# Sign convolutions by halves of images, weight sums one block later, and another order in attention

## The chip, the cores and the metric

One core of one Trainium2 chip runs the whole program. The metric is the device time of a run in microseconds (us), lower is better. TensorE (PE in the profile) multiplies matrices, with its weight loads on a row of their own (PEld). VectorE (DVE), ScalarE (ACT) and GpSimd (POOL) work element by element. SyncE (SP) issues most transfers.

## The reference, cut to what matters

Four layers run one after the other on 16 images of 256 channels and 28 x 28 points, all in float32.

```python
# layer 0: convolution of signs with signs of weights, scaled, normalised, plus the input
out = _binary_activation(x)                              # forward value: sign(x)
scaling = jnp.mean(jnp.abs(weights), axis=(1, 2, 3))
bw = jnp.sign(weights)                                   # forward value
y = _sat_conv2d(out, bw, padding=1, stride=1) * scaling.reshape(1, -1, 1, 1)
# mean and variance over batch and points, then yn * gamma + beta + x

# layer 1: residual block: 3x3 convolution of signs with real weights, 1x1 convolution, two gates

# layer 2: batchnorm, sign, binconv, prelu, batchnorm, sign, binconv, prelu, batchnorm
sf = jnp.mean(jnp.abs(w), axis=(1, 2, 3), keepdims=True) # in each binconv
bw = sf * jnp.sign(w)

# layer 3: self-attention over the 784 points, then
out = jnp.einsum('cr,brn->bcn', Wp, out)
return out.reshape(B, C, H, W) + x
```

Three sign convolutions (one in layer 0, two in layer 2) need signs of 256 x 256 x 9 weights and the mean of their absolute values. The signs go into the convolution; the means are wanted only at the normalisation after it.

## The kernel before: the parts the change touches

The program runs in five stages: sign convolution 1 (layer 0), the residual stage (layer 1), sign convolutions 2 and 3 (layer 2), attention.

A sign convolution works on blocks of 16 rows. The images lie below each other in a ring of three, each followed by one row of zeros that is the lower border of one and the upper border of the next. So 16 images are 16 x 29 = 464 rows, or 29 blocks of 16 x 28 = 448 columns, and a block may begin in one image and end in the next. A block has 23 matmuls: 15 with packed weights (both halves of the output channels in one number), 6 plain ones for the last chunk of weights, and 2 that unpack.

```python
BR = 16
BN = BR * S                      # S = 28
NBLK = B * (S + 1) // BR         # 29
...
for j in range(NBLK + 1):
    if j == 0:
        sign_image(0)
    if j < NBLK:
        packed(j)                # 15 matmuls; then ScalarE and VectorE round the sum
    if j > 0:
        plain(j - 1)             # 6 matmuls, then 2 that unpack
        post(j - 1, pss[j - 1], parts(j - 1))
    ...                          # signs of the next images, as soon as the ring has room
    if j >= 2 and steps:
        steps.pop(0)()
```

`post` takes the block's statistics, in as many pieces (`parts`) as it touches images: VectorE's `bn_stats`, ScalarE's conversion, per piece. `steps` holds work on weights, one step a block. In sign convolution 1 these are seven steps that prepare the weights of the residual stage and six sums of its own weights. In sign convolution 2 they are one sum of its own and the signs and sums of the six weight chunks of sign convolution 3. (Its other sums are taken in the residual stage, where GpSimd does the adding up.) A sum is:

```python
V.tensor_reduce(ab, st.rearrange("p t o -> p o t"), AX.X, ALU.add, apply_absolute_value=True)
part = acc.tile([P, 2], F32, tag="sm", name="sumabs")
for mo in range(2):                               # sums over the partitions, on TensorE
    T.matmul(part[:, mo:mo + 1], lhsT=ab[:, mo * P:(mo + 1) * P], rhs=ones, start=True, stop=True)
V.scalar_tensor_tensor(total, part, 1.0 / K9, total, ALU.mult, ALU.add)
```

The orders on TensorE, ScalarE and VectorE are those of the program (a manual schedule). In attention, image b begins with `project(b - 2, 0)`, `scores(b, 1)`, `scores(b, 2)`; each `scores` is two matmuls and an exponential on ScalarE, with two PSUM buffers in turn. (The timelines count four instructions, x4, for the two matmuls of a sum, of a `scores` or of a `project`.) `take_values(b)`, a ScalarE copy, ends the image.

## Time and profile before

The stages are cut where the first matmul of the next stage starts in TensorE's timeline; "attention" is counted from its first scores (its first projections, from 970.68 us on, are in the row above) to the end.

| | us |
|---|---|
| run, median (1281.66 to 1283.36) | 1282.2 |
| sign convolution 1 | 200.1 |
| residual stage | 401.8 |
| sign convolution 2 | 212.9 |
| sign convolution 3 | 163.4 |
| attention | 302.2 |

Sign convolutions 2 and 3 have the same matmuls, and one takes 49.5 us longer. That is the first thing a table by stage shows.

### The profile page before, as it was taken

How to read it: one execution, taken by the hardware profiler on the slowest of the kernel's cores; microseconds unless marked ns; L12 is line 12 of the kernel's file. 1: busy time of each engine (PE TensorE's matmuls, PEld its weight loads, DVE VectorE, ACT ScalarE, POOL GpSimd, SP SyncE). 2: the span in 40 equal slices, each digit the busy share in tenths (PEclk: the TensorE clock that was granted, in tenths of full speed). 3: DMA queues.
4: the chain of work that ended last, by engine and by line, in shares of the span. 5: the costliest groups of instructions: out<-in, count | busy, mean ns of one | idle time of the engine just before them, and what ended most of it. 6: DMA issues, size and time to landing. Idle time of an engine off the chain costs nothing.

```text
span 1280.3 us, 15397 instructions
## 1 busy us (share of the span) xinstructions
PE 1158.5 (90%) x5808; PEld 931.2 (73%) x5812; DVE 818.1 (64%) x1539; ACT 711.3 (56%) x1067; POOL 137.4 (11%) x137
## 2 busy tenths in 40 slices
PE   6967999999999999985665999999999999999996
PEld 5856888999989999973554888688885545555452
DVE  2833348899999999964334566566666456555655
ACT  4632544676666765655323454455547766776653
POOL 1000000010000000000000000000001432433232
PEclk9978999999999999997877999999999999999998
DMA  7531422133222221103701000000001354445511
GB/s 285 177 136 38 151 91 78 61 113 101 67 110 76 84 103 54 48 29 154 284 25 52 25 1 1 1 1 1 1 1 63 89 151 139 126 114 151 151 77 78
DMA packets 25968, 111.61 MB, mean 87 GB/s; under 512 B 3552, under 2 KB 6304, under 8 KB 25888
## 3 DMA queue, kind: packets, MB, share of 16 engines
q1 hardware_dynamic: 20432, 80.85, 18.2%
q0 software_dynamic: 5456, 29.71, 7.9%
q8 instruction: 48, 0.79, 0.3%
q14 instruction: 32, 0.26, 0.1%
HBM read 65.59 MB, written 44.96 MB: 86 GB/s over the span
## 4 chain that ended last, share of the span: by engine, by line
PE 61%; DVE 13%; ACT 8%; issue 2%; POOL 1%; DMA 0%; ACTq 0%; DVEq 0%; POOLq 0%
PE cv L243 21%; PE cv L567 14%; PE av L992 6%; PE sc L971 6%; PE mi L956 3%; PE sm L1032 3%; PE mi L1042 2%; PE cv L262 2%; DVE p L811 1%; DVE x L696 1%; ACT y L642 1%; DVE x L651 1%; DVE l_parts L698 1%; ACT rn L527 1%; DVE xs L559 1%
## 5 line engine op out<-in xcount | busy, mean ns | idle before, releaser
L243 PE MATMUL cv<-ring,wpk 128*128 128x448 f32 x1305 | 324.7, 405 | 18.7 <-DVE unpack L394 8.8
L567 PE MATMUL cv<-vs,w 128*128 128x392 f32 x1536 | 303.2, 356 | 9.1 <-DVE y L600 7.2
L243 PEld LDWEIGHTS cv<-ring,wpk 128*128 128x128 f32 x1305 | 268.8, 208 | 57.1 <-issue 11.6
L567 PEld LDWEIGHTS cv<-vs,w 128*128 128x128 f32 x1536 | 287.9, 191 | 13.2 <-DVE y L600 10.0
L254 ACT ACTIVATE t<-cv,rounding 128x448 f32<-128x448 f32 x87 | 54.9, 631 | 167.1 <-PE cv L243 167.1
L811 DVE SCALAR_TENSOR_TENSOR p<-r,r,cv 128x448 f32<-128x448 f32 (+15 forms) x172 | 87.1, 506 | 80.2 <-ACT r L806 80.2
L243 PE MATMUL cv<-ring,wpl 128*128 128x448 f32 x522 | 126.6, 379 | 0.0
L255 DVE TENSOR_SCALAR up<-t 128x448 fp32r<-128x448 f32 x87 | 34.0, 391 | 144.5 <-ACT t L254 144.4
L975 ACT ACTIVATE es<-sc 112x784 f32<-112x784 f32 x112 | 87.3, 822 | 61.4 <-PE sc L971 61.3
L243 PEld LDWEIGHTS cv<-ring,wpl 128*128 128x128 f32 x522 | 99.4, 190 | 13.5
L971 PE MATMUL sc<-q,k 64*112 64x392 f32 x448 | 90.6, 518 | 6.2 <-ACT es L975 4.4
L806 ACT ACTIVATE r<-cv 128x896 f32<-128x896 f32 (+1 forms) x60 | 53.4, 893 | 57.7 <-PE cv L262 55.5
L992 PE MATMUL av<-es,va 112*64 112x392 f32 x448 | 80.8, 500 | 0.0
L963 DVE COPY k<-mi 64x784 f32<-64x784 f32 x16 | 15.6, 976 | 93.3 <-ACT q L962 93.3
L971 PEld LDWEIGHTS sc<-q,k 64*112 64x112 f32 x448 | 36.3, 174 | 47.9 <-ACT es L975 16.6
L110 DVE TENSOR_TENSOR vs<-pad 128x840 fp32r<-128x840 bf16 (+1 forms) x68 | 64.1, 975 | 0.6 <-ACT pad L538 0.5
L992 PEld LDWEIGHTS av<-es,va 112*64 112x64 f32 x448 | 29.4, 136 | 47.6 <-issue 44.8
L473 ACT CAST n<-cv 128x896 int16<-128x896 f32 (+15 forms) x43 | 27.7, 645 | 60.7 <-DVE l_parts L472 57.8
L211 PE MATMUL sumabs<-ones,ab 128*128 128x1 f32 x52 | 10.9, 313 | 55.7 <-DVE ab L208 55.7
L985 POOL TENSOR_TENSOR sum<-sum,es 112x784 f32<-112x784 f32 x32 | 60.4, 1887 | 2.5
L664 PE MATMUL cv<-z,fw 128*128 128x392 f32 x256 | 52.4, 355 | 5.1 <-ACT z L655 5.0
L681 ACT ACTIVATE u<-cv,c_bn,s_bn 128x784 f32<-128x784 f32 x31 | 31.1, 1004 | 46.3 <-PE cv L664 46.3
(229 smaller groups left out, 1702.8 us busy)
## 6 DMA issues: line engine op xcount, KB each, us to landing
xs<-in_x_dram SPq DMA_DIRECT2D x32, 784.0 KB, 4.4
x2d<-x POOLq DMA_DIRECT2D x16, 784.0 KB, 3.6
xd<-p SPq DMA_DIRECT2D x16, 784.0 KB, 3.3
out_dram<-p SPq DMA_DIRECT2D x15, 784.0 KB, 5.2
p<-x2d SPq DMA_DIRECT2D x13, 784.0 KB, 15.9
p<-x2d POOLq DMA_DIRECT2D x13, 784.0 KB, 9.0
n0d<-n POOLq DMA_DIRECT2D x16, 392.0 KB, 2.6
n<-n0d SPq DMA_DIRECT2D x16, 392.0 KB, 3.2
```

What stands on the lines that cost most here:

```text
L110: V.tensor_tensor(o, a, b, op)
L243: T.matmul(pss[j][:, mo, :BN].rearrange("p (a b) -> p a b", b=S), lhsT=lhsT, rhs=ring[:, k, r:r + BR, c:c + S], start=start, stop=stop, sk ...
L254: A.activation(r, pss[j][:, 0, :BN], AF.Identity, bias=rounding, scale=1.0 / PACK)
L567: T.matmul(ps.rearrange("p (a b) -> p a b", b=S), lhsT=w[:, k, c, u, mo * P:(mo + 1) * P], rhs=vs[:, b % 2, u, k, :, c:c + S], start=(n == 0),
L664: T.matmul(ps[:, h, :HN], lhsT=w[:, k, mo * P:(mo + 1) * P], rhs=z2[b][:, k, h * HN:(h + 1) * HN], start=(n == 0), stop=(n == 3),)
L806: A.activation(r[:, mo], ps[:, mo, :BN], AF.Relu, scale=-1.0)
L811: V.scalar_tensor_tensor(p, r[:, mo, p0:p0 + n], beta[:, mo:mo + 1], ps[:, mo, p0:p0 + n], ALU.mult, ALU.add)
L956: T.matmul(ps[:, h, :HN], lhsT=wqk[:, k, :], rhs=x[b][:, k, h * HN:(h + 1) * HN], start=(k == 0), stop=(k == 1),)
L971: T.matmul(ps[:MC, h, :HN], lhsT=k_[rows, c * MC:(c + 1) * MC], rhs=qs[b][rows], start=True, stop=True)
L975: A.activation(e, ps[:MC, :, :HN], AF.Exp, scale=0.125)
L985: (V if late else nc.gpsimd).tensor_tensor(sums[b, late], sums[b, late], e, ALU.add)
L992: T.matmul(ps[64 * h:64 * h + 64, :HN], lhsT=w, rhs=e[:, h, :], start=start, stop=stop)
```

## The change

It has three parts. Blocks become halves of images: two buffers with a padded image each take the place of the ring, and 32 blocks of 392 columns that of 29 of 448. Sums of weights come in two steps: VectorE's part in one block, TensorE's part (and the total) one block later. In attention, scores 1 goes ahead of the projection, and the `take_values` of the image before moves behind its exponential.

```diff
-    def ring_tile(pool, tag):
-        t = pool.tile([P, 2, RROWS + BR + 2, S + 2], FR, tag=tag, name="ring")
+    def float_pads(pool, tag):
+        t = pool.tile([P, 2, 2, S + 2, S + 2], FR, tag=tag, name="fpads")
 ...
                 V.tensor_reduce(ab, st.rearrange("p t o -> p o t"), AX.X, ALU.add, apply_absolute_value=True)
+            return lambda: total_up(k, g, ab)
+
+        def total_up(k, g, ab):
             part = acc.tile([P, 2], F32, tag="sm", name="sumabs")
 ...
-            for j in range(NBLK + 1):
+            for j in range(2 * B + 1):
                 if j == 0:
                     sign_image(0)
-                if j < NBLK:
+                if j < 2 * B:
                     packed(j)
                 if j > 0:
                     plain(j - 1)
-                    post(j - 1, pss[j - 1], parts(j - 1))
+                    post(j - 1, pss[j - 1])
+                if j == 0:
+                    sign_image(1)
+                elif j % 2 == 0 and j // 2 + 1 < B:
+                    sign_image(j // 2 + 1)
 ...
-                if j >= 2 and steps:
-                    steps.pop(0)()
+                if late:
+                    late()
+                late = steps.pop(0)() if j >= 2 and steps else None
 ...                                    (the same two lines in the residual stage; then post of layer 0)
-                for at, b, r0, r1, p0 in parts:
-                    n = (r1 - r0) * S
 ...
-                    for mo in range(2):
-                        V.bn_stats(mom.part(at, mo), ps[:, mo, p0:p0 + n])
-                    A.copy(ns[b][:, :, r0 * S:r1 * S], ps[:, :, p0:p0 + n])
 ...
+                for mo in range(2):
+                    V.bn_stats(mom.part(j, mo), ps[:, mo, :HN])
+                A.copy(ns[b][:, :, h * HN:(h + 1) * HN], ps[:, :, :HN])
 ...                                    (attention)
+            scores(b, 1)
+            if b > 0:
+                take_values(b - 1)
             if b > 1:
                 project(b - 2, 0)
-            scores(b, 1)
             sum_up(b, 1)
             scores(b, 2)
 ...
-                take_values(b)
                 if b > 0:
                     normalize(b - 1)
```

More of the change, by code (lines that the diff above doesn't have):

```diff
@@ L46 @@
 EPS = 1e-5
-BR = 16
-BN = BR * S
-NBLK = B * (S + 1) // BR
-RING = 3
-RROWS = RING * (S + 1)
 PACK = 4095.0
@@ L91, in conv_seq_kernel @@
     nc.gpsimd.memset(ones, 1.0)
-    def ring_tile(pool, tag):
-        t = pool.tile([P, 2, RROWS + BR + 2, S + 2], FR, tag=tag, name="ring")
-        nc.gpsimd.memset(t[:, :, 0::S + 1, :].bitcast(F32), 0.0)
-        for c in (0, S + 1):
-            nc.gpsimd.memset(t[:, :, :, c:c + 1].bitcast(F32), 0.0)
+    def float_pads(pool, tag):
+        t = pool.tile([P, 2, 2, S + 2, S + 2], FR, tag=tag, name="fpads")
+        for i in (0, S + 1):
+            nc.gpsimd.memset(t[:, :, :, i:i + 1, :].bitcast(F32), 0.0)
+            nc.gpsimd.memset(t[:, :, :, :, i:i + 1].bitcast(F32), 0.0)
         return t
@@ L221, in run @@
             f()
-            s()
+            return s()
         return [lambda f=f, s=s: run(f, s) for f, s in zip(first, second)]
@@ L230, in split2, with sign_layer @@
         tt(dsts[1], st, dsts[0].bitcast(F32), ALU.subtract)
-    def sign_layer(ring, w, temp, sign, post, steps, moments):
-        pss = [None] * NBLK
-        bs = [None] * NBLK
+    def sign_layer(pads, w, temp, sign, post, steps, moments):
+        pss = [None] * 2 * B
+        bs = [None] * 2 * B
         def product(j, mo, lhsT, n, t, start, stop, again=False):
@@ L241, in product @@
             r, c = divmod(3 * g + t, 3)
-            r += BR * j % RROWS
+            r += HR * (j % 2)
             T.matmul(
-                pss[j][:, mo, :BN].rearrange("p (a b) -> p a b", b=S), lhsT=lhsT,
-                rhs=ring[:, k, r:r + BR, c:c + S], start=start, stop=stop, skip_group_check=again,
+                pss[j][:, mo, :HN].rearrange("p (a b) -> p a b", b=S), lhsT=lhsT,
+                rhs=pads[:, j // 2 % 2, k, r:r + HR, c:c + S], start=start, stop=stop, skip_group_check=again,
             )
@@ L253, in packed @@
             r, bs[j] = temp("t1"), temp("up", FR)
-            A.activation(r, pss[j][:, 0, :BN], AF.Identity, bias=rounding, scale=1.0 / PACK)
+            A.activation(r, pss[j][:, 0, :HN], AF.Identity, bias=rounding, scale=1.0 / PACK)
             V.tensor_scalar(bs[j], r, -ROUND, None, ALU.add)
@@ L262, in plain @@
                 T.matmul(
-                    pss[j][:, mo, :BN], lhsT=unpack[mo], rhs=bs[j], start=False, stop=True, skip_group_check=(mo == 0)
+                    pss[j][:, mo, :HN], lhsT=unpack[mo], rhs=bs[j], start=False, stop=True, skip_group_check=(mo == 0)
                 )
-        count = 0
-        def parts(j):
-            nonlocal count
-            at, out = BR * j, []
-            while at < BR * (j + 1):
-                i, r0 = divmod(at, S + 1)
-                r1 = min(S, r0 + BR * (j + 1) - at)
-                if r1 > r0:
-                    out.append((count, i, r0, r1, (at - BR * j) * S))
-                    count += 1
-                at += max(r1 - r0, 1) if r0 < S else 1
-            return out
-        def sign_image(i):
-            at = i % RING * (S + 1) + 1
-            for r0, r1 in ((0, BR + 1), (BR + 1, S)) if i == 0 else ((0, S),):
-                sign(i, slice(r0, r1), lambda k: ring[:, k, at + r0:at + r1, 1:S + 1])
-            if i and i % RING == 0:
-                sign(i, slice(0, BR + 1), lambda k: ring[:, k, RROWS + 1:RROWS + BR + 2, 1:S + 1])
-        done = 0
+        def sign_image(i):
+            for r0, r1 in ((0, HR + 1), (HR + 1, S)) if i == 0 else ((0, S),):
+                sign(i, slice(r0, r1), lambda k: inner(pads[:, i % 2], k, r0, r1))
+        late = None
         with tc.manual_schedule(engines={ET.PE, ET.Activation, ET.DVE}):
-            for j in range(NBLK + 1):
+            for j in range(2 * B + 1):
                 if j == 0:
                     sign_image(0)
-                if j < NBLK:
+                if j < 2 * B:
                     packed(j)
@@ L296, in sign_layer @@
                     plain(j - 1)
-                    post(j - 1, pss[j - 1], parts(j - 1))
-                if j == NBLK - 2:
-                    moments.gather()
-                while done + 1 < B and (j == 0 if done + 1 < RING else (done + 1 - RING) * (S + 1) + S <= BR * j - 1):
-                    done += 1
-                    sign_image(done)
-                if j >= 2 and steps:
-                    steps.pop(0)()
-        assert done == B - 1 and not steps
+                    post(j - 1, pss[j - 1])
[3 more added lines that the diff above has]
+                    sign_image(j // 2 + 1)
+                if j == 2 * B - 2:
+                    moments.gather()
+                if late:
+                    late()
+                late = steps.pop(0)() if j >= 2 and steps else None
+        assert not steps and not late
     def inner(pad, k, r0=0, r1=S):
@@ L318, in combine, with halves_moments @@
         return v
-    EARLY = NBLK + B - 2 - 3
-    EARLY_COUNT = sum(o % (S + 1) < S for o in range(BR * (NBLK - 2))) * S
-    def sign_moments(name):
-        return Moments(name, EARLY, 3, EARLY_COUNT)
+    def halves_moments(name):
+        return Moments(name, 2 * B - 3, 3, (2 * B - 3) * HN)
     sf0, sf1, sf2 = vtile("sf0"), vtile("sf1"), vtile("sf2")
@@ L356, in conv_seq_kernel @@
         with tc.tile_pool(name="ph1", bufs=1) as ph:
-            ring = ring_tile(ph, "vs")
+            fpads = float_pads(ph, "vs")
             w0[1] = plain_weights(ph, tag="z2", bufs=1)
@@ L375, in temp @@
             def temp(tag, dt=F32):
-                return ph.tile([P, BN], dt, tag=tag, name=tag, bufs=2)
+                return ph.tile([P, HN], dt, tag=tag, name=tag, bufs=2)
             def quarter(tag):
-                return temp(tag)[:, 0:HN]
+                return temp(tag)
             signs, sums_ = sign_weights(ph, w0, d["w0"], sf0, pss, ("yu", 6))
@@ L465, in conv_seq_kernel, with post0 @@
             steps = [lambda k=k, c=c: w1_step(k, c) for k in range(2) for c in range(3)] + [fw_step] + sums_ + [constants]
-            def post0(j, ps, parts):
-                for at, b, r0, r1, p0 in parts:
-                    n = (r1 - r0) * S
-                    if r0 == 0:
-                        ns[b] = ph.tile([P, 2, N], I16, tag="n", name=f"n{b}", bufs=2)
-                    for mo in range(2):
-                        V.bn_stats(mom.part(at, mo), ps[:, mo, p0:p0 + n])
-                    A.copy(ns[b][:, :, r0 * S:r1 * S], ps[:, :, p0:p0 + n])
-                    if r1 == S:
-                        nc.gpsimd.dma_start(out=n0d[b], in_=ns[b])
-            mom = sign_moments("l0")
-            sign_layer(ring, w0, temp, sign0, post0, steps, mom)
+            def post0(j, ps):
+                b, h = divmod(j, 2)
+                if h == 0:
+                    ns[b] = ph.tile([P, 2, N], I16, tag="n", name=f"n{b}", bufs=2)
+                for mo in range(2):
+                    V.bn_stats(mom.part(j, mo), ps[:, mo, :HN])
+                A.copy(ns[b][:, :, h * HN:(h + 1) * HN], ps[:, :, :HN])
+                if h == 1:
+                    nc.gpsimd.dma_start(out=n0d[b], in_=ns[b])
+            mom = halves_moments("l0")
+            sign_layer(fpads, w0, temp, sign0, post0, steps, mom)
             load_x(0, True)
@@ L707, in conv_seq_kernel @@
             mom1 = Moments("l1", 2 * B - 4, 4, (B - 2) * N)
+            late = None
             enter(0)
@@ L762, in conv_seq_kernel @@
                     prelu_out(b, 1)
-                if b >= 2 and steps:
-                    steps.pop(0)()
+                if late:
+                    late()
+                late = steps.pop(0)() if b >= 2 and steps else None
         ppool = ctx.enter_context(tc.tile_pool(name="ppool", bufs=1))
@@ L773, in conv_seq_kernel @@
             w2a[1] = plain_weights(ph, tag="wal")
-            ring = ring_tile(ph, "ring")
+            fpads = float_pads(ph, "fpads")
             def temp(tag, dt=F32):
-                return ph.tile([P, BN], dt, tag=tag, name=tag, bufs=2)
+                return ph.tile([P, HN], dt, tag=tag, name=tag, bufs=2)
             rest = [x[5] for x in sign_weights(ph, w2a, d["w2a"], sf1, pss, ("r", 2), ab_tag="ab")]
@@ L801, in post2, with post @@
             def post2(order, beta, mom):
-                def post(j, ps, parts):
-                    r = ph.tile([P, 2, BN], F32, tag="r", name="r", bufs=2)
-                    for mo in (slice(0, 1), slice(1, 2)) if j == NBLK - 1 else (slice(0, 2),):
-                        A.activation(r[:, mo], ps[:, mo, :BN], AF.Relu, scale=-1.0)
-                    for at, i, r0, r1, p0 in parts:
-                        n = (r1 - r0) * S
-                        for mo in range(2):
-                            p = pt[order[i]][:, mo, r0 * S:r1 * S]
-                            V.scalar_tensor_tensor(
-                                p, r[:, mo, p0:p0 + n], beta[:, mo:mo + 1], ps[:, mo, p0:p0 + n], ALU.mult, ALU.add
-                            )
-                            V.bn_stats(mom.part(at, mo), p)
+                def post(j, ps):
+                    i, h = divmod(j, 2)
+                    r = ph.tile([P, 2, HN], F32, tag="r", name="r", bufs=2)
+                    for mo in (slice(0, 1), slice(1, 2)) if j == 2 * B - 1 else (slice(0, 2),):
+                        A.activation(r[:, mo], ps[:, mo, :HN], AF.Relu, scale=-1.0)
+                    for mo in range(2):
+                        p = pt[order[i]][:, mo, h * HN:(h + 1) * HN]
+                        V.scalar_tensor_tensor(p, r[:, mo], beta[:, mo:mo + 1], ps[:, mo, :HN], ALU.mult, ALU.add)
+                        V.bn_stats(mom.part(j, mo), p)
                 return post
             steps = [rest[1]] + both(*sign_weights(xpool, w2b, d["w2b"], sf2, pss, ("x2", 3), tmp=ph, ab_tag="ab"))
-            mom = sign_moments("l2b")
+            mom = halves_moments("l2b")
             sign_layer(
-                ring, w2a, temp, lambda i, rows, out: sign2(x2[order[i]], sg1, bg1, rows, out), post2(order, r1, mom), steps, mom
+                fpads, w2a, temp, lambda i, rows, out: sign2(x2[order[i]], sg1, bg1, rows, out), post2(order, r1, mom), steps, mom
             )
@@ L824, in conv_seq_kernel @@
             sg2, bg2 = norm("l2b", mom, pv("g2"), pv("b2"), sf1)
-            mom = sign_moments("l2c")
+            mom = halves_moments("l2c")
             sign_layer(
-                ring, w2b, temp, lambda i, rows, out: sign2(pt[i], sg2, bg2, rows, out), post2(range(B), r2, mom), [], mom
+                fpads, w2b, temp, lambda i, rows, out: sign2(pt[i], sg2, bg2, rows, out), post2(range(B), r2, mom), [], mom
             )
```

## The prediction

> **What bounds the kernel now.** I read the page's busy shares first (TensorE 90%, VectorE 64%, ScalarE 56%), then the chain that ended last (TensorE 61% of it; the sign convolutions, L243 and L262, are its largest part), then TensorE's waits by releaser, then its timeline. Whatever shortens TensorE's stream shortens the run. Its waits, in us in total, times, longest:
> ```profile
> PE sumabs L211 <- DVE ab L208: 55.7, 13, 5.7
> ...
> PE sc L971 <- ACT es L975: 4.4, 16, 0.3
> ...
> PE sumabs L211 <- POOL st L205: 3.4, 4, 1.1
> ```
> One line dwarfs the rest: 13 tiny products that sum weights wait for VectorE. TensorE's timeline in the second sign convolution (start, length), first a stretch with such sums, then one without:
> ```profile
> 636.35 5.58 PE L243 MATMUL cv<-ring,wpk 128*128 128x448 f32 x15
> 641.76 1.46 PE L243 MATMUL cv<-ring,wpl 128*128 128x448 f32 x6
> 643.06 0.57 PE L262 MATMUL cv<-up,unpack 128*128 128x448 f32 x2
> 649.25 0.98 PE L211 MATMUL sumabs<-ones,ab 128*128 128x1 f32 x4 [5.62 <-DVE ab L208]
> 650.10 5.53 PE L243 MATMUL cv<-ring,wpk 128*128 128x448 f32 x15
> ...
> 716.30 3.37 PE L243 MATMUL cv<-ring,wpk 128*128 128x448 f32 x15
> 719.51 1.45 PE L243 MATMUL cv<-ring,wpl 128*128 128x448 f32 x6
> 720.80 0.57 PE L262 MATMUL cv<-up,unpack 128*128 128x448 f32 x2
> 721.21 3.39 PE L243 MATMUL cv<-ring,wpk 128*128 128x448 f32 x15
> ```
> An undisturbed block of 23 matmuls takes 4.91 us (716.30 to 721.21), a block with a sum 13.75 us (636.35 to 650.10). The wait is 5.62 us of the difference; the rest is that the 15 matmuls after it take 5.5 instead of 3.2 us, and the sum's own 0.9. The same two stretches, in busy time, clock and DMA:
> ```profile
> 612.40:711.40 99.00, 62.20 (x214) 53.80 (x213) 35.98 (x81) 26.93 (x34) 0.00 (x0) 0.76 0.29 106
> 711.40:795.00 83.60, 83.60 (x392) 73.99 (x391) 52.32 (x117) 46.87 (x58) 0.00 (x0) 1.00 0.00 1
> ```
> After the length come TensorE, weight loads, VectorE, ScalarE and GpSimd, then the clock. TensorE is busy 62 of 99 us at a mean clock of 0.76, then fully at 1.00; VectorE and ScalarE are under half busy in the first. So no engine is short there: it is an ordering loss.
>
> **What the Trainium skill says.** (1) "TensorE: Matmul & The Clock Gate", Part 3, The mechanism: matmuls run in strict order. The trace agrees: ready convolution matmuls stand 5.62 us behind one sum of two columns. (2) Same page, Part 1, What's actually happening: after an idle window of about 3.4 us the array runs at half clock. Agreed: the clock is 0.50 in 624 to 628 us, and 15 matmuls take 5.5 instead of 3.2 us. (3) Same page, Back-to-back issue gap: an isolated gap of N/2.4 + 2.5 ns, 189 ns for N = 448 and 166 for 392, while it gives 131 ns for N = 512 in a stream with weight loads. The trace has 4.91/23 = 213 ns for 448, so I take the trace's figures. (4) "DMA: Bandwidth & Descriptors", Where 436 GB/s comes from: a ceiling near 435 GB/s. The trace shows 408 to 433 GB/s from 600 to 628 us, so loads there can't come sooner.
>
> **The change, part by part.**
> 1. *Halves of images.* 29 blocks of 448 columns become 32 of 392 per layer; 23 matmuls each stay. The 392-column price is in the first residual convolution (L567): 49 in 9.27 us (311.52 to 320.79), 189 ns. A block is 23 x 0.189 = 4.35 us, a layer 32 x 4.35 = 139.2 against 29 x 4.92 = 142.7; three layers save **10 us**. The 3% fewer columns is all of it: more instructions at nearly the same price per column.
> 2. *Second block no longer needs image 1.* Block 1 of 16 rows reached into the next image, so its signs were on TensorE's path: 1.65 us before the second block in both later layers, 1.52 in the first. Half an image doesn't: **5 us**.
> 3. *Sums one block later, first layer.* Block starts 60.80 to 120.53 are 59.7 us for 6 blocks worth 29.5; 30.2 lost. A sum itself stays, 0.45 us warm (82.21 to 82.68), 2.7 in all. **27.5 us.**
> 4. *Sums one block later, second sign layer.* 612.36 to 711.36 is 99.0 us for 8 blocks worth 39.4; 59.6 lost, less 7 sums at 0.45: 56.5 us to win. But something is uncovered. The next layer's weights are loaded in the queue behind 13 images, and the first weight load, issued at 613.57, landed 15.6 us later, at 629.2. Before, ScalarE first touched them at 631.3, late enough. After, with blocks of 4.35 us from the same start (601.9), TensorE reaches the first delayed sum of these weights at 601.9 + 2.85 x 2 + 1.5 + 3 x 4.35 = 622.1. Its operand needs the load (629.2), ScalarE's sign (0.83), VectorE's packing (0.54) and its reduction (1.02): 631.6. A wait of some 9.5 us, once, and then cold matmuls, about 2.5 us. **56.5 - 12 = 44.5 us.**
> 5. *Weight preparation of the residual convolution, within layer 1's sign blocks.* Seven blocks carry 4 ScalarE and 8 VectorE operations. They already take 5.09 us (25.16 to 60.80 for seven) because ScalarE and VectorE wait for each other. I expect about 4.9 rather than the 4.35 of item 1, so I take back **3.5 us**.
> 6. *GpSimd's sums in the residual stage* had 3.4 us of waits; VectorE is busy 225 of 240 us there and will absorb part: **2 us**.
> 7. *Attention.* ScalarE's order is exponential 0, take values, exponential 1; TensorE waits 0.27 us for exponential 1 in 16 images. With scores 1 ahead of the projection, exponential 1 starts about 0.7 us sooner and the projection's 0.76 us fills the wait: 16 x 0.27 = **4.3 us**.
> 8. *Layer ends*: 29 instead of 40 gathered statistics, fewer pieces: **1 us**.
>
> Sum: 10 + 5 + 27.5 + 44.5 - 3.5 + 2 + 4.3 + 1 = 90.8 us. 1282.2 - 90.8 = **1191 us**.
>
> **Rivals.**
> *The weight load takes the place of the wait* (item 4). For it: DMA runs at its ceiling until 628 us, the queue's order is the same in the built changed kernel, and the delayed sum stands in front of ready matmuls. Against: only the first weights are so late; the next needs only 3 us to land. I count it at 12 us. If the load isn't waited for (another order of landing), the run is 1179.
> *VectorE becomes the bound of the blocks with sums.* For it: in the second layer a block carries about 0.36 + 2.4 + 0.54 + 1.02 + 0.16 = 4.5 us of VectorE work (two multiply-adds and two statistics at 0.6 each, packing, reduction, total). Against: such a block lasts 4.35 + 0.45 = 4.8 us on TensorE. If VectorE's latencies add 0.8 us to each of 13 blocks, 10 us go: 1201.
> *Two image buffers instead of a ring of three starve TensorE.* The signs of image i+1 may start only when image i-1 is done and must end one block later. In the first layer that is statistics 1.04, conversion 0.8, signs 1.6, with gaps 3.9 us, in 4.35. If it failed by 0.5 us in 14 images of the first layer, 7 us would go. In the others the chain is about 3.0 us: no danger.
> *All of it hidden elsewhere*, for instance the waits only move to the next wait: against it speaks that after 711 us the same engines run the same blocks with TensorE 100% busy.
>
> **Range and chances.** Items 3 and 4 carry four fifths; what can fail is the size of the uncovered load wait (0 to 20 us) and of VectorE's backlog (0 to 10), while item 1 may be 7 to 15. That gives 1177 to 1208. "Within 2%" (above 1256.5) would need both large items to fail, so 2.5%.
>
> **What would show each step right or wrong.** TensorE's waits for `ab` fall from 55.7 us to one or two, of which the longest, near 622 to 632 us less what earlier stages won, goes back to the landing of weights. Blocks of the third sign layer take 4.35 us. In blocks with sums TensorE's clock is 1.0 save after that wait. The waits of scores for exponentials fall below 1 us. Wrong would be: 392-column matmuls in the sign layers at over 200 ns; waits of L243's successor for the signs of an image in every second block; a first layer whose preparation blocks take over 5.3 us; or sums that wait for VectorE in most blocks as now.

## More of the kernel before

`conv_ps` gives a block one of three PSUM buffers.

On the profile's page, the line of busy shares, and the slices in time of TensorE and of its granted clock (each digit is a fortieth of the span, in tenths):

```profile
PE 1158.5 (90%) x5808; PEld 931.2 (73%) x5812; DVE 818.1 (64%) x1539; ACT 711.3 (56%) x1067; POOL 137.4 (11%) x137
...
PE   6967999999999999985665999999999999999996
PEclk9978999999999999997877999999999999999998
```

TensorE is at nine tenths nearly everywhere, save for two dips, in slices 3 and 4 and in slices 18 to 22, and there the clock falls too. Slices 3 and 4 and slices 20 to 22 are where weights are summed; slices 18 and 19 (544 to 608 us) hold the end of the residual stage.

## The result, and the profile after

The changed kernel takes 1179.2 us (1178.6 to 1180.0, four runs) against 1282.2: 103 us less. The ratio is 0.920, with a 95% interval of 0.918 to 0.921. Here and below a ratio is the mean time of one kernel's fast runs over that of the other's of the same rounds, so not quite the ratio of the medians.

| stage, us | before | after | less | predicted less |
|---|---|---|---|---|
| sign convolution 1 | 200.1 | 164.7 | 35.5 | 29.2 |
| residual stage | 401.8 | 398.9 | 2.9 | 2 |
| sign convolution 2 | 212.9 | 161.1 | 51.8 | 49.9 |
| sign convolution 3 | 163.4 | 156.0 | 7.3 | 5.4 |
| attention | 302.2 | 297.6 | 4.6 | 4.3 |

The predicted column puts the items of the prediction into stages: for sign convolution 1, 3.4 of columns + 1.5 + 27.5 - 3.5 + 0.3. Each column rests on one profile. How far one profile differs from another shows in e3 (below): sign convolutions 1 and 2, which e3 doesn't touch, took 1.5 and 3.0 us longer in its profile than in that of the kernel before. The page's busy shares, and its slices in time:

```profile
PE 1113.0 (94%) x6015; PEld 944.0 (80%) x6019; DVE 817.7 (69%) x1438; ACT 692.3 (59%) x1041; POOL 142.7 (12%) x139
...
PE   6999999999999999994889999999999999999995
PEclk9999999999999999996989999999999999999998
```

The first dip is gone; of the second two slices at eight tenths are left (20 and 21, 559.6 to 618.6 us). The slice at four tenths before them (530.2 to 559.6 us) is the end of the residual stage. VectorE has as much work as before, 818 us, in 101 fewer instructions. TensorE's waits by releaser (us in total, times, longest):

```profile
PE cv L543 <- DVE y L576: 10.6, 11, 1.2
...
PE sumabs L207 <- DVE ab L201: 8.9, 1, 8.9
...
PE sc L946 <- ACT es L950: 0.7, 2, 0.3
```

The 13 waits for `ab` have become one, the waits of scores for exponentials have nearly gone, and GpSimd's sums aren't waited for any more. TensorE's timeline in sign convolution 2 around the one wait that is left (start, length, instructions, and in brackets the wait ahead of them):

```profile
584.14 0.52 PE L258 MATMUL cv<-up,unpack 128*128 128x392 f32 x2
593.52 1.01 PE L207 MATMUL sumabs<-ones,ab 128*128 128x1 f32 x4 [8.87 <-DVE ab L201]
594.40 4.68 PE L239 MATMUL cv<-fpads,wpk 128*128 128x392 f32 x15
598.92 1.30 PE L239 MATMUL cv<-fpads,wpl 128*128 128x392 f32 x6
600.05 0.52 PE L258 MATMUL cv<-up,unpack 128*128 128x392 f32 x2
600.41 0.50 PE L207 MATMUL sumabs<-ones,ab 128*128 128x1 f32 x4
600.77 3.08 PE L239 MATMUL cv<-fpads,wpk 128*128 128x392 f32 x15
```

And ScalarE's timeline at the same time:

```profile
591.09 0.84 ACT L189 ACTIVATE sg<-st 128x768 bf16<-128x768 f32 x1 [10.54 <-DMA st<-in_w2b_dram]
```

The wait goes from ScalarE's sign, which had to wait 10.54 us for the weight load, over VectorE's packing and reduction to TensorE's sum. It came where the prediction put it: 21.1 us after the stage's first matmul at 563.52 (predicted 20.2), 8.9 us long (predicted some 9.5). The matmuls behind it took 4.68 instead of 3.08 us. The next sum, at 600.41, waits for nothing, and the blocks with sums behind it last 4.8 to 5.1 us.

Sign convolution 2 in two stretches, with the weight work and behind it, and then sign convolution 3 (columns as in the prediction):

```profile
563.50:624.97 61.47, 52.48 (x274) 50.84 (x274) 34.23 (x71) 29.16 (x39) 0.00 (x0) 0.92 0.64 244
624.97:716.00 91.03, 91.03 (x484) 90.62 (x484) 56.23 (x107) 48.26 (x62) 0.00 (x0) 1.00 0.00 1
724.60:861.00 136.40, 136.39 (x724) 135.77 (x725) 79.82 (x152) 73.33 (x95) 0.00 (x0) 1.00 0.00 1
```

In the stretch with weights TensorE is idle for 9.0 of 61.5 us, which is the one wait; behind it for none. In the last two stretches no wait is left that another order could take away. Its weight loads are busy nearly all the time there too (135.8 of 136.4 us).

The start of sign convolution 3 before, then after, from TensorE's timeline:

```profile
819.97 3.78 PE L243 MATMUL cv<-ring,wpk 128*128 128x448 f32 x15 [1.65 <-ACT ring L789]
```

```profile
724.61 6.04 PE L239 MATMUL cv<-fpads,wpk 128*128 128x392 f32 x30
```

Before, the second block waited for the signs of image 1. After, the first two blocks stand in one row of 30 matmuls.

Attention, the beginning of an image, before and after:

```profile
1050.24 1.48 PE L971 MATMUL sc<-q,k 64*112 64x392 f32 x8
1051.99 0.92 PE L971 MATMUL sc<-q,k 64*112 64x392 f32 x4 [0.27 <-ACT es L975]
```

```profile
968.33 0.92 PE L946 MATMUL sc<-q,k 64*112 64x392 f32 x4
969.08 0.82 PE L1017 MATMUL mi<-o,wp 64*128 64x392 f32 x4
969.74 1.48 PE L946 MATMUL sc<-q,k 64*112 64x392 f32 x8
```

Scores 3 had to wait 0.27 us for exponential 1. After, the projection stands between scores 1 and 2, and scores 2 and 3 follow without a gap.

### The profile page after: what moved, and what is told of

Same layout as the page of the kernel before. It is cut to its first block, busy times and chain, and to the rows that moved or that the text cites. A ratio compares the mean times of both kernels' runs of the same rounds, so it can differ in the third digit from the quotient of the medians.

```text
span 1178.2 us, 15695 instructions
## 1 busy us (share of the span) xinstructions
PE 1113.0 (94%) x6015; PEld 944.0 (80%) x6019; DVE 817.7 (69%) x1438; ACT 692.3 (59%) x1041; POOL 142.7 (12%) x139
## 3 DMA queue, kind: packets, MB, share of 16 engines
q1 hardware_dynamic: 20432, 80.85, 19.6%
## 4 chain that ended last, share of the span: by engine, by line
PE 64%; DVE 14%; ACT 3%; DMA 2%; issue 1%; SPq 0%; DVEq 0%; ACTq 0%
PE cv L239 20%; PE cv L543 16%; PE sc L946 7%; PE av L967 6%; PE mi L931 4%; PE sm L1007 4%; DVE x L672 2%; DVE x L627 2%; DVE l_parts L674 2%; DVE xs L535 2%; PE cv L258 2%; PE mi L1017 2%; DVE y L576 1%; DMA st<-in_w2b_dram 1%; DMA p<-x2d 1%
## 5 line engine op out<-in xcount | busy, mean ns | idle before, releaser
L543 PE MATMUL cv<-vs,w 128*128 128x392 f32 x1536 | 302.3, 355 | 11.4 <-DVE y L576 10.6
L239 PE MATMUL cv<-fpads,wpk 128*128 128x392 f32 x1440 | 295.3, 358 | 12.5 <-DVE wpk L190 10.0
L239 PEld LDWEIGHTS cv<-fpads,wpk 128*128 128x128 f32 x1440 | 273.2, 193 | 17.3 <-issue 10.4
L788 DVE SCALAR_TENSOR_TENSOR p<-r,r,cv 128x392 f32<-128x392 f32 x128 | 78.6, 614 | 80.4 <-ACT r L785 80.4
L239 PE MATMUL cv<-fpads,wpl 128*128 128x392 f32 x576 | 124.8, 352 | 0.0
L239 PEld LDWEIGHTS cv<-fpads,wpl 128*128 128x128 f32 x576 | 108.8, 190 | 0.6
L250 ACT ACTIVATE t<-cv,rounding 128x392 f32<-128x392 f32 x96 | 56.2, 586 | 86.5 <-PE cv L239 81.7
L251 DVE TENSOR_SCALAR up<-t 128x392 fp32r<-128x392 f32 x96 | 35.0, 364 | 84.4 <-ACT t L250 84.4
L785 ACT ACTIVATE r<-cv 128x784 f32<-128x784 f32 (+1 forms) x66 | 52.9, 805 | 60.0 <-PE cv L258 58.1
L449 ACT CAST n<-cv 128x784 int16<-128x784 f32 x32 | 26.0, 813 | 54.7 <-DVE l_parts L448 24.1
L640 PEld LDWEIGHTS cv<-z,fw 128*128 128x128 f32 x256 | 46.9, 193 | 5.6 <-ACT z L631 5.5
```

Of the source, the lines that this page charges most:

```text
L239: T.matmul(pss[j][:, mo, :HN].rearrange("p (a b) -> p a b", b=S), lhsT=lhsT, rhs=pads[:, j // 2 % 2, k, r:r + HR, c:c + S], start=start, s ...
L250: A.activation(r, pss[j][:, 0, :HN], AF.Identity, bias=rounding, scale=1.0 / PACK)
L543: T.matmul(ps.rearrange("p (a b) -> p a b", b=S), lhsT=w[:, k, c, u, mo * P:(mo + 1) * P], rhs=vs[:, b % 2, u, k, :, c:c + S], start=(n == 0),
L640: T.matmul(ps[:, h, :HN], lhsT=w[:, k, mo * P:(mo + 1) * P], rhs=z2[b][:, k, h * HN:(h + 1) * HN], start=(n == 0), stop=(n == 3),)
L785: A.activation(r[:, mo], ps[:, mo, :HN], AF.Relu, scale=-1.0)
L788: V.scalar_tensor_tensor(p, r[:, mo], beta[:, mo:mo + 1], ps[:, mo, :HN], ALU.mult, ALU.add)
```

## The experiments

All six kernels gave correct results. Runs e1 to e4 share one chip and its nine runs of the kernel before (median 1283.1 us), e5 and e6 another (1282.4 us).

### e1: the late sums alone

The edit, on the kernel before: the two-step sum and the two `late` places, with ring and attention as they were.

```diff
+            return lambda: total_up(k, g, ab)
...
-                if j >= 2 and steps:
-                    steps.pop(0)()
+                if late:
+                    late()
+                late = steps.pop(0)() if j >= 2 and steps else None
```

> The kernel before with the late sums alone (all stages). My account: 27.5 us in the first layer, 2.9 us in the residual stage, and in the second sign layer 56.5 us less one wait for the late weight load, which with blocks of 4.92 us should be about 4.5 us (not 8.9): 51 us. Sum 81 us, 1201 us. TensorE's waits for ab fall from 55.7 us to one of about 4.5 us. Rival: the sums only pay because halves of images shorten the work of VectorE and ScalarE per block; then waits stay and less than 60 us are won.

Measured: 1203.5 us, ratio 0.938 (0.936 to 0.939), 80 us less. Sign convolution 1 takes 174.7 us (25.4 less) and sign convolution 2 162.8 (50.1 less). Two lines of its profile, from TensorE's waits and from its timeline in sign convolution 2:

```profile
PE sumabs L214 <- DVE ab L208: 2.5, 3, 2.1
...
603.86 0.88 PE L214 MATMUL sumabs<-ones,ab 128*128 128x1 f32 x4 [2.07 <-DVE ab L208]
```

The waits for `ab` are down to three with 2.5 us in total. So the sums pay without the halves, and by the predicted amount: this part alone is the bulk of the change. The load is late here as well (ScalarE stands 4.45 us for it), but TensorE, with longer blocks and a cold second block, comes to its sum later and waits 2.07 us, not the 4.5 that I had expected.

### e2: the halves alone

The edit, on the changed kernel: the total at once, and (not shown) attention in the old order.

```diff
-            return lambda: total_up(k, g, ab)
+            total_up(k, g, ab)
```

> The changed kernel with the sums taken at once and attention in the old order, so halves of images alone. My account: 10 us of columns, 8 us at the three starts of layers, 2 us at layer ends, less a longer wait for the late weight load (about 9 us more than its sum waited before): 1271 us, between 1262 and 1278. Rival: halves carry a large part of the 103 us themselves (fewer pieces for VectorE and ScalarE), then below 1250.

Measured: 1249.4 us, ratio 0.975 (0.973 to 0.977), 34 us less, where I had expected 12. The expectation failed in two terms above all. The wait for the late load isn't longer: the stage's first sum, of its own weights, waits 4.3 us first, so TensorE reaches the second when the load has nearly landed. And the waits themselves are shorter. TensorE's waits in this run:

```profile
PE sumabs L207 <- DVE ab L201: 48.5, 13, 5.1
```

They were 55.7 us. By stage, sign convolution 1 is 10.2 us shorter, 2 is 13.8 us shorter and 3 is 7.3 us shorter; the third has neither sums nor weight work, so its 7.3 us are halves alone.

Why a block of halves is followed by a shorter wait had no experiment of its own, but the trace of the kernel before answers much of it. In sign convolution 1, VectorE takes the statistics of a block ahead of its sum, in one piece or in two. A sum behind two pieces, then one behind one piece:

```profile
91.17 0.58 PE L211 MATMUL sumabs<-ones,ab 128*128 128x1 f32 x4 [3.34 <-DVE ab L208]
...
100.50 0.58 PE L211 MATMUL sumabs<-ones,ab 128*128 128x1 f32 x4 [2.28 <-DVE ab L208]
```

Behind two pieces TensorE waits 3.2 to 3.3 us there, behind one (save for the first sum) 2.1 to 2.3. With halves every block has one piece, and the wait in e2 is 2.1 to 2.2 us (again save for the first).

The parts don't add: 80 + 34 + 5 is 119, and the whole is 103. By stage, 12 of the 16 us that are counted twice lie in sign convolution 2: halves win 13.8 us there alone, and only 1.7 on top of the late sums (162.8 in e1, 161.1 in the changed kernel), while in sign convolutions 1 and 3 they win the same either way (10.2 or 10.1, and 7.3). Two things make up most of the 12. The late load costs more when both parts are there: a wait of 8.9 and 1.6 us of slow matmuls, against 2.1 and 1.2 in e1, so 7.2 more. And the sums' waits in this stage, which late sums take away anyhow, are 3.6 us shorter with halves (33.2 instead of 36.8).

### e3: attention alone

The edit, on the kernel before, is the last part of the diff above.

> The kernel before with the attention order alone: 4.3 to 4.6 us won, 1277.7 us; TensorE's waits of scores for exponentials fall from 4.4 us in 16 to under 1 us, one iteration from 18.13 to 17.86 us. Rival: the gain comes from elsewhere, then the attention stage is 302 us long as before.

Measured: 1277.7 us, ratio 0.9964 (0.995 to 0.998). That is 4.6 us less by the ratio, 5.4 by the medians. The attention stage takes 297.8 us instead of 302.2, and the waits of scores for exponentials fall from 4.4 us in 16 to 0.7 us in 2. The gain is the small waits, as predicted. The interval lies wholly below 1, so the small gain is real.

### e4: weight steps of sign convolution 2 begun three blocks later

The edit, on the changed kernel:

```diff
-    def sign_layer(pads, w, temp, sign, post, steps, moments):
+    def sign_layer(pads, w, temp, sign, post, steps, moments, first=2):
...
-                late = steps.pop(0)() if j >= 2 and steps else None
+                late = steps.pop(0)() if j >= first and steps else None
...
-                fpads, w2a, ..., post2(order, r1, mom), steps, mom
+                fpads, w2a, ..., post2(order, r1, mom), steps, mom, 5
```

> The changed kernel with the weight steps of the second sign layer begun three blocks later (from block 5, not 2), so that the first delayed sum comes after its weights have landed. If the 8.9 us wait and the slow matmuls after it (1.6 us) come from that load, both go: 10.5 us, 1168.7 us, and no wait for ab is left. Rival: the wait is VectorE's or ScalarE's backlog and only moves: 1179 us, with the wait three blocks later.

Measured: 1169.6 us, ratio to before 0.912 (0.911 to 0.914); the changed kernel has 0.920, so 9 to 10 us less. Sign convolution 2 takes 151.2 instead of 161.1 us. TensorE's timeline at the first two sums:

```profile
593.49 0.61 PE L207 MATMUL sumabs<-ones,ab 128*128 128x1 f32 x4
593.95 3.07 PE L239 MATMUL cv<-fpads,wpk 128*128 128x392 f32 x15
...
598.95 0.61 PE L207 MATMUL sumabs<-ones,ab 128*128 128x1 f32 x4 [0.42 <-DVE ab L201]
```

The longest wait for `ab` is 0.4 us and the three together are 1.2 us; the matmuls behind the sums keep 3.1 us. Had the wait been a backlog of VectorE or ScalarE, it would have come again three blocks later. So it was the load, and the cold matmuls were its follow-up. This version beats both kernels.

### e5: TensorE kept busy ahead of the waiting sums

The edit, on the kernel before: matmuls whose result nobody reads, ahead of each sum's own.

```diff
+            if fill:                  # 9 in sign convolution 1, 20 in sign convolution 2
+                keep_busy(fill)
             part = acc.tile([P, 2], F32, tag="sm", name="sumabs")
```

> The kernel before with matmuls of no use put ahead of each waiting sum (20 in the second sign layer, 9 in the first: some 4.3 and 1.9 us of the wait at 215 ns each). The sums still wait until VectorE is done; TensorE is only kept busy meanwhile. If half the clock after the wait is due to idleness, the 15 matmuls after a sum fall from 5.5 to 3.3 us and the sum from 0.9 to 0.5: 7 x 2.8 us in the second sign layer and some 5 us in the first, 25 us, 1258 us, with idle time before sums down to 1 us each. Rival: the clock falls for another reason, or the 15 matmuls are slow because of VectorE; then 1283 us or more.

Measured: 1261.7 us, ratio 0.984 (0.982 to 0.986), 21 us less (25 expected). The interval lies below 1. TensorE's timeline around a sum of sign convolution 2 of this run:

```profile
624.09 4.49 PE L356 MATMUL unused<-idle 128*128 128x512 bf16 x20
629.41 0.58 PE L213 MATMUL sumabs<-ones,ab 128*128 128x1 f32 x4 [0.84 <-DVE ab L208]
629.85 3.48 PE L245 MATMUL cv<-ring,wpk 128*128 128x448 f32 x15
```

The sum comes no sooner after its block. But the 15 matmuls behind it take 3.48 us, where the same ones in the kernel before took 5.6. More work made the kernel faster by 21 us. So more than a quarter of what e1 won in the two stages (25.4 + 50.1 = 75.5 us) was not waiting but the slow clock after it. The trace of the kernel before agrees: the thirteen groups of 15 matmuls behind its sums take, from first start to the start of what follows, 21.9 us more than 3.3 us each, which is what they take at full speed. Sign convolution 2 alone gains 13.4 us of the 19.6 expected. One reason is in the trace: its first two blocks ran colder in this run (4.92 and 5.23 us for 15 matmuls), and one block in the middle was still slow (4.86 us). The cold start isn't the edit's: from the stage's first matmul to its third block this run takes 13.3 us, and so does e3, which has no such matmuls, where the kernel before took 10.5.

### e6: statistics of sign convolution 1 in two pieces

The edit, on the changed kernel; only the number of pieces changes:

```diff
-                for mo in range(2):
-                    V.bn_stats(mom.part(j, mo), ps[:, mo, :HN])
-                A.copy(ns[b][:, :, h * HN:(h + 1) * HN], ps[:, :, :HN])
+                for q in range(2):
+                    s = slice(q * HN // 2, (q + 1) * HN // 2)
+                    for mo in range(2):
+                        V.bn_stats(mom.part(2 * j + q, mo), ps[:, mo, s])
+                    A.copy(ns[b][:, :, h * HN + q * HN // 2:h * HN + (q + 1) * HN // 2], ps[:, :, s])
```

> The changed kernel with statistics and conversion of the first layer in two pieces per block, as most blocks of the kernel before had them. If the pieces (statistics and conversion of the first wait for each other ahead of the second) made the weight-preparation blocks 5.09 us long, these go from 4.58 back towards 4.9 to 5.1 us, 8 of them, and in plain blocks the signs of every second block come too late by some 0.3 us: 3 to 8 us slower than the changed kernel, 1182 to 1187 us. Rival: only the smaller blocks and the three PSUM buffers count; then 1179 to 1180 us.

Measured: 1188.1 us, ratio to before 0.927 (0.926 to 0.929), so 9 us slower than the changed kernel. Sign convolution 1 takes 171.8 instead of 164.7 us. TensorE's timeline in the blocks that prepare weights:

```profile
39.57 3.28 PE L239 MATMUL cv<-fpads,wpk 128*128 128x392 f32 x15 [1.28 <-ACT fpads L348]
...
44.71 3.12 PE L239 MATMUL cv<-fpads,wpk 128*128 128x392 f32 x15 [0.37 <-ACT n L451]
...
50.60 3.29 PE L239 MATMUL cv<-fpads,wpk 128*128 128x392 f32 x15 [1.27 <-ACT fpads L348]
```

Two such blocks take 11.03 us (39.57 to 50.60), 5.5 each, more than I had expected. In VectorE's timeline the second piece's statistics wait 0.60 us for ScalarE's conversion of the first:

```profile
43.50 0.64 DVE L450 BATCH_NORM_STATS2 l_parts<-cv 128x6 f32<-128x196 f32 x2 [0.60 <-ACT n L451]
```

Both only read the buffer; why one waits for the other wasn't tested. Five blocks pay 4.3 of the 7.1 us for this, and 2.2 us are at the layer's end, where VectorE gathers twice as many statistics (3.3 instead of 1.7 us for the gathering). This is more than a step back to the kernel before, against what the expectation says: that kernel's ScalarE made 43 conversions for 29 blocks, so 14 of its blocks had two pieces; here all have. In plain blocks nothing waits, against my expectation of 0.3 us in every second one.

## Why the prediction was right, point by point

The time of 1179.2 us lies in the range (1177 to 1208), near its lower end and 12 us below the point. The bulk (items 3 and 4) was right in cause and size. By the table of stages 11 us more were won than predicted, and they are in small terms: by one profile each, columns some 3.5, the starts of layers 2.5, their ends 1.8, weight preparation 1.5 and the load's wait 1.5. One agreement is chance: the prediction names 1179 us for the case that the weight load is not waited for. It was waited for, 8.9 us.

1. **Columns (10 us).** Undersized. In sign convolution 3, where nothing waits behind the second block, a block took 4.93 us before (825.28 to 953.44 for 26) and takes 4.33 now (731.98 to 857.45 for 29), not 4.92 and 4.35. A layer saves 29 x 4.93 - 32 x 4.33, by the unrounded values 4.5 us instead of 3.5. The price per matmul is 188 ns.
2. **Start of the layers (5 us).** Undersized. From the first matmul to the third block, sign convolution 3 went from 10.5 to 7.4 us, where the 1.65 us wait and 38 cheaper matmuls make 2.6 of the 3.1. In sign convolution 1 the third block starts 4.3 us sooner instead of some 2.5: I left out that the second block, after its wait, had run cold (its 15 matmuls took 5.9 us). With the ring this stretch also scatters: in sign convolution 2 it took 10.5, 11.9, 13.3 and 13.3 us in the four kernels that have it (the one before, e1, e3, e5), and 7.3 in each of the four with halves.
3. **Late sums of sign convolution 1 (27.5 us).** Six blocks with sums now take 28.9 us, 4.8 each as predicted. e1 gives 25.4 us for the stage with the late sums alone, and there one wait of 1.64 us for signs takes the place of the first.
4. **Late sums of sign convolution 2 and the weight load (56.5 - 12).** The wait is 8.9 and the cold matmuls 1.6 us, together 10.5 where I had 12. e4 removes both and gains 9.9 us in the stage. This is the rival that I had taken into the sum; it came about as named.
5. **Weight preparation (3.5 us taken back).** Too much, and from a line misread. I expected 4.9 us a block (whose own product, 7 x 0.55, is 3.9); the trace has 4.58 (eight blocks from 20.84 to 57.44), with two waits of 0.5 us for signs, so it took back 8 x 0.25 = 2.0 us. The 5.09 us of before were no floor set by ScalarE and VectorE: 4.92 of them were TensorE's own matmuls, and its waits in those seven blocks were 0.44 and 0.19 us. e6 shows what could have set one: with two pieces in every block the same work takes 5.5 us. The change had removed the second pieces, and I had not priced that.
6. **GpSimd's sums (2 us).** The 3.4 us of waits went, and TensorE's waits for `y` rose from 7.2 to 10.6 us, exactly as much, also in e1. The stage's 2.9 us are partly scatter: without late sums it took 401.8, 400.3, 400.1 and 399.9 us in four kernels, with them 398.9, 399.3, 400.0 and 399.4. The means differ by 1.1 us. The wait mostly moved, as I had half expected.
7. **Attention (4.3 us).** 4.6 us, confirmed by e3.
8. **Layer ends (1 us).** Undersized. From the last matmul of a sign convolution to the first of the next stage it was 8.6, 7.5 and 17.5 us in the three layers, and is 7.1, 6.6 and 17.0, together 2.8 us less. Which of fewer statistics and an earlier last transfer did it was not tested.

The rivals: VectorE didn't become the bound (no wait for `ab` but the one). The two image buffers starved TensorE in two blocks of sign convolution 1 only, by 0.5 us each. The waits for `ab` didn't move elsewhere; only GpSimd's did (item 6).

Four readings of the kernel before were loose, without harm to the sums. The clock of 0.50 stands in 622 to 627 us; in the next us it is 0.68. The 15 matmuls behind a sum took 5.4 us from first start to what follows, against 3.2 (5.5 was their length; by length the others take 3.4). The transfers ran at 411 to 427 GB/s in stretches of 4 us from 600 to 628; the 435 GB/s of the prediction's point (4) is the figure that the Trainium skill's page gives for the fabric ("DMA: Bandwidth & Descriptors", Where 436 GB/s comes from), and that it is what limits these loads is not shown. And the trace agrees with point (2) only in part: 15 matmuls also took 4.9 us after waits of 3.34 us (at 91.61) and of 2.28 us (at 100.94), both shorter than the idle window of some 3.4 us that the Trainium skill gives ("TensorE: Matmul & The Clock Gate", Part 1, What's actually happening), but 3.5 us after another of 2.28 us (at 120.53).

One thing I didn't foresee is how large the share of the halves is when they stand alone (34 us, e2). After the late sums they are worth 1203.5 - 1179.2 less attention's 4.6, about 20 us.

## What to carry to other kernels

When a small product on TensorE needs the end of another engine's chain, and nobody needs its result soon, issue it one block later: here 13 sums of about half a microsecond each cost some 75 us, more than a quarter of that through the slow clock after the waits. After such a change look for what used to land in time only because the program was slow: here a weight load, worth another 10 us by starting its users three blocks later. And count pieces, not only elements: with a second piece of statistics that waited for another engine's reading of the first, the blocks that prepare weights took 5.5 us instead of 4.6 (e6), while plain blocks, with time to spare, took no longer.

## What the Trainium skill lacked or had wrong

- "TensorE: Matmul & The Clock Gate", Back-to-back issue gap: neither of its two figures holds for float32r streams with one weight load per matmul. The page has N/2.4 + 2.5 ns (166 ns for N = 392, 189 for 448) or about 131 ns for N = 512 in a stream with weight loads; the runs show 188 ns for 392 columns and 214 for 448 (means over sign convolution 3, after and before).
- Same page, Part 1: it tells of the slow clock after idle windows, but puts no price on filling a wait with matmuls that nobody reads. Here 194 of them, in 13 waits, gained 21 us (e5).
